# A two-layer transformer kernel on one core: layer 0 with two tiles for low parts, the key bias in the keys' tile, and chain matmuls queued behind the last score

## The chip, the core and the metric

The kernel runs on one core of one Trainium2 chip. A core has several engines, each with its own instruction queue that it works off in order: TensorE (PE in the profile; PEld is its weight load), VectorE (DVE), ScalarE (ACT), GpSimd (POOL) and SyncE (SP), which here issues most of the DMAs. The metric is device time in microseconds of the slowest core; with one core that is the time of the launch. Lower is better.

## The reference

The input `x` is 16 batches of 512 tokens of 128 features, in float32. Two layers follow each other, each of them a half FFN, an attention, and a half FFN again. The change lies in layer 0 alone:

```python
x = x + 0.5 * L0_ffn(layernorm(x))     # silu(gate) * up, inner width 352; all operands
                                       # quantized to 4-bit floats in blocks of 16
x = x + L0_attn(layernorm(x))          # 16 heads of 8; relative positions clipped to +-64
x = x + 0.5 * L0_ffn(layernorm(x))
...                                    # layer 1: another FFN (with experts) and a linear attention

def L0_attn(x):
    dist = clip(k - q, -64, 64) + 64
    q, k, v = heads(x @ W_qkv + b_qkv);  q = q / sqrt(8)
    score = q @ k.T + einsum(q, rel_emb_k[dist])
    attn  = softmax(score, axis=-1)
    ctx   = attn @ v + einsum(attn, rel_emb_v[dist])
    return ctx @ W_out + b_out
```

## The kernel before

**Scores.** A batch is worked in two halves of 256 queries; a half-batch is called a unit here, and its number is u = 2b + half, from 0 to 31. A score tile holds 128 keys by 32 queries of all 16 heads: 128 x 512 numbers in one PSUM tile named `sps`, of which there are three. A unit has 32 such tiles. Each is made twice: once by `maxima`, where VectorE reduces it at once to its maximum over the keys (L341, into `mx`), and once by `main`, where ScalarE takes the exponential (L369, into `PT`). The two lie one unit apart: while `main` works on unit u, `maxima` works on unit u + 1. When its 32 tiles are through, `maxima` gathers the maxima over the tiles (`mk`, L347), turns them on TensorE (L349, also into an `sps` tile), and reduces and negates them on VectorE (L351, L352). The result goes to DRAM (`MD`, L353) and from there into one row of the operand tile `a_BD` (four DMAs, L355), so that the second score comes out with its maximum already subtracted. A score tile is four products of float16 operands (L263: `a_KS` holds the keys, `a_BD` the queries, each as a high and a low part so that the sum has float32's accuracy) and, where the positions are within the clipped range, eight small ones for the relative positions (L267, with `a_TQ` and `a_ET`).

**Projections.** `prep` normalizes a batch, turns it (L282), and makes queries (z = 0) and keys (z = 1) with one product each (L286). Each result is split into a high and a low float16 part by `f16split`: VectorE casts (L143, tile `qkhi`, two buffers), GpSimd subtracts (L144, tile `qklo`, one buffer). Of the queries' parts, copies go into `a_HM` (L298) and from there by twelve DMAs to DRAM (`QM`, L300); high and low parts go by three DMAs each to `QS` and `KSd` (L302). Then the bias that the keys at the clipped distances get is computed from the queries (L305), split by VectorE (L307: `rhi` takes a `qkhi` buffer, `rlo` the `qklo` tile), and stored in `QS` by four DMAs (L309). All of these are on SP's queue for every batch but the first. `loadK` and `load` bring the operands of a unit back on chip in the arrangement that the scores want (L315, L329, L330); they are issued in the middle of the maxima of the unit before.

**What follows the scores.** `main` multiplies the exponentials with the values (L272, L274, into `av`) and with the relative embeddings (`rps`), sends the latter through DRAM to reorder them (`RV`, `RD`, `a_cr`) and copies the former to `cx` (L412). `fin` adds both (L422), turns the sum (L430, four transposes into one `mps` tile; PSUM has two `mps` tiles), divides by the softmax's sum (L433, L434), turns again (L437), multiplies by the output weights (L440) and adds the residual. The FFN halves (`FFN.half`, called `head` ahead of the attention and `tail` behind it) are a chain of the same kind: normalize, quantize (L70 to L81, on VectorE and GpSimd), transpose (L115), two products for each half (L121, L125), quantize, transpose (L133), product (L139).

**Order.** All these are Python generators, and `interleave` runs a step of that one whose due time comes first: `S` in `layer0` lists for each its number of steps and the unit times at which it begins and ends (for example `part`, the stream of maxima, 33 steps per unit; `main` 59 steps; `fin` 5; `head` and `tail` 21; `prep` 11). `prep` runs two batches ahead and `head` three. The tile framework then schedules the traced instructions on each engine by its own timeline; `high_priority` moves an instruction up, and `issue_after(x)` keeps those traced inside it behind x in their engine's queue. Before the main loop, the maxima of unit 0 (`mxs(0,0)`), `FFN1.pre`, `head(1)`, `prep(1)`, the first 14 steps of unit 1's maxima and `head(2)` are traced in this order.

The tile pool `wk` has one buffer for each name unless `bufs` says otherwise, and tiles of one name use the same space in turn: the next use waits until all who read the last one are done. `xn` is such a name too: the normalized batch, then the keys, both [128, 4, 128] float32. `xk` holds the batches' residuals, in seven tiles; `xl` loads one (L474), `tail` stores it (L487) when it is done.

Of the kernel before, what the change touches and what calls it, by code (L numbers as in the profile page):

```python
# [8 lines left out]
F32 = mybir.dt.float32  # L9
F16 = mybir.dt.float16  # L10
# [15 lines left out]
class K:  # L26
# [57 lines left out]
class FFN:  # L84
# [22 lines left out]
    def half(f, xb, half, wk, pp):  # L107
# [6 lines left out]
        ps=pp.tile([128,512],F32,name="mps")  # L114
        for j in range(2): nc.tensor.transpose(ps[:,j*128:(j+1)*128],xq[:,j*128:(j+1)*128],s.ident)  # L115
        xqT=wk.tile([128,256],F32,name="f_x",bufs=3); nc.scalar.copy(xqT,ps[:,:256]); yield
        h=wk.tile([128,2,I],F32,name="f_h")
        for j in range(2):
            t=h[:,j,:]
            g=pp.tile([128,512],F32,name="mps")  # L120
            nc.tensor.matmul(g[:,:I],xqT[:,j*128:(j+1)*128],f.wguT[:,0,:],start=True,stop=True)  # L121
# [3 lines left out]
            nc.tensor.matmul(u[:,:I],xqT[:,j*128:(j+1)*128],f.wguT[:,1,:],start=True,stop=True)  # L125
            nc.vector.scalar_tensor_tensor(t,u[:,:I],0.5,t,ALU.mult,ALU.mult); yield
        for hq in s.quant_steps(h.rearrange("p a b -> p (a b)"),wk,128,44,"hq"): yield
        hq=hq.rearrange("p (a b) -> p a b",a=2)
        for j in range(2):
            ps=pp.tile([128,512],F32,name="mps")  # L130
            for c in range(3):
                P=min(128,I-c*128)
                nc.tensor.transpose(ps[:P,c*128:(c+1)*128],hq[:,j,c*128:c*128+P],s.ident)  # L133
            hT=wk.tile([128,3,128],F32,name="hT",bufs=1)
            nc.scalar.copy(hT[:,0:2,:],ps[:,:256])
            nc.scalar.copy(hT[:96,2,:],ps[:96,256:384])  # L136
            for c in range(3):
                P=min(128,I-c*128)
                nc.tensor.matmul(ps[:,384:512],hT[:P,c,:],f.wdT[:P,c,:],start=(c==0),stop=(c==2),skip_group_check=True)  # L139
            nc.vector.scalar_tensor_tensor(xh[:,j,:],ps[:,384:512],0.5,xh[:,j,:],ALU.mult,ALU.add); yield  # L140
# [5 lines left out]
class Attn0:  # L146
# [110 lines left out]
    def scores(a, out, kt, half, b, BD, TQ, KS):  # L257
# [4 lines left out]
        for g in range(4):  # L262
            nc.tensor.matmul(o4[:,g],KS[:,sd,g*512+kt*128:g*512+(kt+1)*128],BD[:,g,:,b*32:b*32+32].rearrange("p h (x j) -> p x h j",j=4),start=(g==0),stop=(not ib and g==3),skip_group_check=True)  # L263
        if ib:
            for x in range(8):
                w0=kt*128-blk*32-x+a.OFF
                nc.tensor.matmul(out[:,x*64:x*64+64],a.ET[:,w0:w0+128],TQ[:,:,b*32+4*x:b*32+4*x+4],start=False,stop=(x==7),skip_group_check=True)  # L267

# [6 lines left out]
    def prep(a, b, xb, wk, pM):  # L275
# [5 lines left out]
        ps=pM.tile([128,512],F32,name="mps")  # L281
        for j in range(4): nc.tensor.transpose(ps[:,j*128:(j+1)*128],xn[:,j,:],a.ident)  # L282
        xnT=a.xnT[b]=wk.tile([128,512],F32,name="xnT",bufs=2); nc.scalar.copy(xnT,ps); yield
        for z in range(2):
            ps=pM.tile([128,512],F32,name="mps")
            nc.tensor.matmul(ps,a.w[:,z*128:(z+1)*128],xnT,start=True,stop=True)  # L286
            f=wk.tile([128,512],F32,name="qk0") if z==0 else wk.tile([128,4,128],F32,name="xn").rearrange("p a b -> p (a b)")
# [19 lines left out]
        nc.vector.tensor_copy(rhi,ps[:32]); nc.vector.tensor_tensor(rlo,ps[:32],rhi,ALU.subtract)  # L307
# [24 lines left out]
    def maxima(a, b, half, wk, pS, pM):  # L332
# [83 lines left out]
    def fin(a, b, half, X, wk, pM):  # L416
# [11 lines left out]
        for t in range(2):  # L428
            ps=pM.tile([128,512],F32,name="mps")
            for z in range(4): nc.tensor.transpose(ps[:,z*128:z*128+128],cx[:,z,t*128:t*128+128],a.ident)  # L430
            p3=ps.rearrange("p (h c) -> p h c",c=32)
# [4 lines left out]
        ps=pM.tile([128,512],F32,name="mps")  # L436
        for t in range(2): nc.tensor.transpose(ps[:,t*128:t*128+128],cn[:,t,:],a.ident)  # L437
        ct=wk.tile([128,2,128],F32,name="cn").rearrange("p a b -> p (a b)"); nc.scalar.copy(ct,ps[:,:256])
        ps=pM.tile([128,512],F32,name="mps")
        for t in range(2): nc.tensor.matmul(ps[:,t*128:(t+1)*128],ct[:,t*128:(t+1)*128],a.wo,start=True,stop=True)  # L440
        xh=xb[:,2*half:2*half+2,:]
# [15 lines left out]
def layer0(tc, s, w, src, dst, nb=16):  # L457
# [3 lines left out]
    with ExitStack() as c:  # L461
# [56 lines left out]
        loads(1); ffn2(head,1); run(prep(1)); run(part(14)); ffn2(head,2)  # L518
        S=[(part(99999),33*2*nb,W['part'],2*nb+W['part'])]
        for b in range(nb):  # L520
            for h in range(2):
# [7 lines left out]
                if b+hl<nb: at(head(b+hl,h),21,*W['head'])  # L529
                if h==0 and b+pl<nb: at(prep(b+pl),11,*W['prep'])  # L530
# [509 lines left out]
```

## Time and profile before

| | |
|---|---|
| median of 3 runs | 3613.2 us (3611.74 to 3618.94) |
| the profiled execution, its own time | 3625.44 us |
| its span, first to last instruction | 3623.7 us |
| TensorE busy / VectorE / ScalarE / GpSimd, share of the span | 78% / 67% / 47% / 23% |
| mean granted TensorE clock | 0.897 |
| layer 0: first score to last, in the span | 129.4 to 1971.3 us |
| in that stretch: TensorE busy, VectorE busy, clock | 1620.6 us, 1419.7 us, 0.96 |
| behind it (layer 1): TensorE busy, VectorE busy, clock | 1149.1 us, 965.2 us, 0.84 |
| L341 (maximum of a score tile, VectorE) | 1024 of 702 ns |
| L369 (exponential of a score tile, ScalarE) | 1024 of 598 ns |
| L263 (one of a score tile's four products, TensorE) | 8192 of 222 ns |

One execution was profiled, and all single times come from it; it took 12 us longer than the median of the timed runs. The page of the profile gives busy time by engine, then the span in 40 slices of 90.6 us each, in which a digit is the busy share in tenths; the row PEclk is the clock that TensorE was granted, in tenths of full speed. A row of a list of waits reads: engine, what it was about to write, line, what released it, line; then the idle time in us, the number of waits and the longest. In a timeline a row gives the start, the length, the engine, the line and the operation with what it writes and reads; in brackets at its end stands the idle time before it and what ended that. SPq is the issuing of a DMA on SP's queue.

### The profile page before, as it was taken

How to read it: one execution, taken by the hardware profiler on the slowest of the kernel's cores; microseconds unless marked ns; L12 is line 12 of the kernel's file. 1: busy time of each engine (PE TensorE's matmuls, PEld its weight loads, DVE VectorE, ACT ScalarE, POOL GpSimd, SP SyncE). 2: the span in 40 equal slices, each digit the busy share in tenths (PEclk: the TensorE clock that was granted, in tenths of full speed). 3: DMA queues.
4: the chain of work that ended last, by engine and by line, in shares of the span. 5: the costliest groups of instructions: out<-in, count | busy, mean ns of one | idle time of the engine just before them, and what ended most of it. 6: DMA issues, size and time to landing. Idle time of an engine off the chain costs nothing. (4 is left out here: it accounts for less than half of the span.)

```text
span 3623.7 us, 95110 instructions
## 1 busy us (share of the span) xinstructions
PE 2827.4 (78%) x40077; PEld 2034.6 (56%) x40077; DVE 2441.3 (67%) x6508; ACT 1699.9 (47%) x3391; POOL 828.1 (23%) x789
## 2 busy tenths in 40 slices
PE   5579988889888898889896288873788888888470
PEld 3357776767767676677775144431565555555240
DVE  5567878778877787777773467774546655645367
ACT  3144554545445454545554156533455454445242
POOL 4122222222222222222101222212112211111226
PEclk8689999999999999999998589886899989989785
DMA  3232222322223222222210111104312222121401
GB/s 103 59 94 67 58 53 63 80 63 54 62 68 79 63 49 58 75 71 62 53 33 20 32 33 36 36 28 128 90 54 72 62 59 59 36 62 36 128 15 47
DMA packets 290159, 217.23 MB, mean 60 GB/s; under 512 B 77402, under 2 KB 257476, under 8 KB 289604
## 3 DMA queue, kind: packets, MB, share of 16 engines
q1 hardware_dynamic: 284468, 207.72, 21.5%
q8 instruction: 315, 5.16, 0.6%
q10 hardware_dynamic: 5264, 3.43, 0.4%
q14 instruction: 112, 0.92, 0.1%
HBM read 110.28 MB, written 100.78 MB: 58 GB/s over the span
## 5 line engine op out<-in xcount | busy, mean ns | idle before, releaser
L341 DVE TRANSPOSE_TENSOR_REDUCE mx<-sps 128x16 f32<-128x512 f32 x1024 | 702.6, 702 | 221.4 <-PE sps L263 119.5
L369 ACT ACTIVATE PT<-sps 128x512 f32<-128x512 f32 x1024 | 578.4, 598 | 579.0 <-PE sps L263 335.1
L263 PE MATMUL sps<-a_BD,a_KS 128*128 128x128 f16 x8192 | 746.5, 222 | 115.5 <-DVE mx L341 52.1
L263 PEld LDWEIGHTS <-a_KS 128*128 128x128 f16 x8192 | 552.4, 99 | 289.3 <-issue 249.5
L723 DVE SCALAR_TENSOR_TENSOR moe<-mps,oh,moe 128x128 f32<-128x128 f32 x896 | 289.6, 341 | 117.9 <-PE mps L721 104.1
L267 PE MATMUL sps<-a_TQ,a_ET 128*128 128x64 f16 x7168 | 368.5, 194 | 0.4 <-DMA a_TQ<-QM 0.4
L59 POOL TENSOR_TENSOR ln_rs<-ln_ve,negh 128x4 f32<-128x4 f32 (+1 forms) x192 | 174.6, 919 | 636.6 <-DVE ln_ve L58 545.0
L721 PE MATMUL mps<-f_W,T 128*128 128x512 f32 x512 | 298.1, 701 | 26.0 <-DVE moe L723 21.0
L267 PEld LDWEIGHTS <-a_ET 128*128 128x128 f16 x7168 | 309.2, 99 | 1.6 <-DMA a_TQ<-QM 0.6
L79 POOL TENSOR_TENSOR q_M<-f_h,q_M 128x704 f32<-128x704 f32 x64 | 108.2, 1690 | 715.2 <-DVE f_h L78 507.2
L274 PE MATMUL av<-PT,a_V 128*32 128x256 f32 x3840 | 250.7, 386 | 0.0
L896 DVE TENSOR_TENSOR a_at<-pp,a_cm 128x1024 f32<-128x1024 f32 x128 | 154.2, 1214 | 73.1 <-PE pp L894 72.0
L894 PE MATMUL pp<-a_F 64*128 64x128 f32 x2048 | 165.5, 300 | 41.5 <-DVE a_at L896 29.6
L894 PEld LDWEIGHTS pp<-a_F 64*128 64x128 f32 x2048 | 139.6, 202 | 91.6 <-DVE a_at L896 35.0
L721 PEld LDWEIGHTS mps<-f_W,T 128*128 128x128 f32 x512 | 102.1, 223 | 126.7 <-issue 72.9
L274 PEld LDWEIGHTS av<-PT,a_V 128*32 128x32 f32 x3840 | 120.6, 111 | 68.1 <-issue 3.7
L876 ACT ACTIVATE a_F<-pp 128x1024 f32<-128x1024 f32 x128 | 126.6, 1025 | 50.2 <-PE pp L874 44.0
L62 ACT ACTIVATE xn<-xn,ln_mr,ln_rs 128x128 f32<-128x128 f32 x256 | 103.7, 482 | 93.8 <-DVE ln_mr L60 49.0
L274 PE MATMUL rps<-PT,a_TV 128*32 128x64 f32 x6912 | 134.1, 222 | 5.6 <-issue 5.2
L675 ACT COPY f_PT<-St 32x512 f32<-32x512 f32 x128 | 78.7, 615 | 111.2 <-DVE St L674 106.7
L139 PE MATMUL mps<-wdT,hT 128*128 128x128 f32 (+1 forms) x768 | 122.9, 299 | 4.3 <-ACT hT L136 3.6
L874 PE MATMUL pp<-a_QK,a_PK 128*128 128x512 f16 x256 | 81.3, 406 | 55.8 <-DMA a_QK<-a1d 28.9
(348 smaller groups left out, 5375.8 us busy)
## 6 DMA issues: line engine op xcount, KB each, us to landing
QM<-a_HM SPq DMA_DIRECT2D x180, 128.0 KB
a_TQ<-QM SPq DMA_DIRECT2D x120, 192.0 KB
RD<-RV SPq DMA_DIRECT2D x32, 512.0 KB
a_KS<-KSd SPq DMA_DIRECT2D x128, 96.0 KB
a_QK<-a1d SPq DMA_DIRECT2D x128, 96.0 KB
xn<-X SPq DMA_DIRECT2D x32, 256.0 KB
a1d<-a_hi SPq DMA_DIRECT2D x64, 128.0 KB
a_BD<-QS SPq DMA_DIRECT2D x128, 58.0 KB
```

What stands on the lines that cost most here:

```text
L59: nc.gpsimd.tensor_tensor(rs,ve,s.negh[:,:n],ALU.pow); yield
L139: nc.tensor.matmul(ps[:,384:512],hT[:P,c,:],f.wdT[:P,c,:],start=(c==0),stop=(c==2),skip_group_check=True)
L263: nc.tensor.matmul(o4[:,g],KS[:,sd,g*512+kt*128:g*512+(kt+1)*128],BD[:,g,:,b*32:b*32+32].rearrange("p h (x j) -> p x h j",j=4),start=(g==0 ...
L267: nc.tensor.matmul(out[:,x*64:x*64+64],a.ET[:,w0:w0+128],TQ[:,:,b*32+4*x:b*32+4*x+4],start=False,stop=(x==7),skip_group_check=True)
L274: for p,q in mms[1:]: a.nc.tensor.matmul(*p,**q)
L341: with a.s.tc.high_priority(): r=nc.vector.tensor_reduce(mx[:,kt,:,bb],ps.rearrange("p (i c) -> p i c",c=32),axis=AX.X,op=ALU.max,apply_tr ...
L369: nc.scalar.activation(pt[:,:,bb*32:bb*32+32].rearrange("p h (x j) -> p x h j",j=4),ps.rearrange("p (x h j) -> p x h j",x=8,j=4),AF.Exp)
L721: nc.tensor.matmul(ps,yT[:,j*128:(j+1)*128],a.W[:,e2*4:e2*4+4,:],start=True,stop=True)
L723: nc.vector.scalar_tensor_tensor(moe[:,j,:],ps[:,e*128:(e+1)*128],oh[:,j,e2*4+e:e2*4+e+1],moe[:,j,:],ALU.mult,ALU.add)
L876: nc.scalar.activation(f,ps,AF.Relu)
L894: nc.tensor.matmul(ps[:,hh,bs],f[hh*64:hh*64+64,1,bs],f[hh*64:hh*64+64,0,bs],start=True,stop=True)
L896: nc.vector.tensor_tensor(k,ps.rearrange("p h (b q) -> p (h b) q",b=4),a.cm.unsqueeze(1).to_broadcast([128,8,128]),ALU.mult)
```

## The change

The change has four parts. First, `qklo` has two buffers, and the split key bias (`rhi`, `rlo`) lies in a tile of the name `xn`, as [128, 1024] float16, in place of a `qkhi` buffer and the `qklo` tile. Second, `scores` remembers its last matmul (`s.lastmm`), and a new function `gate()` puts the matmuls of the chains (projections, FFN, `fin`, the transpose of `mk`) behind the last score traced so far in TensorE's queue; the values' product (L319) and those of `main` (L272, L274) are not gated. Third, three `yield`s are added, in the FFN between the copy of `hT` and its product, in `maxima` ahead of the transpose of `mk`, and in `fin` ahead of the output product; the numbers of steps follow. Fourth, `xk` has six tiles where it had seven. The same instructions are issued as before. In the diff the other gated matmuls are left out: in `half` all of L115 to L139, in `prep` L282 too, in `fin` L430, L437 and L440.

```diff
+    lastmm=None
+    def gate(s):
+        return s.tc.issue_after(s.lastmm) if s.lastmm is not None else ExitStack()
...
     def half(f, xb, half, wk, pp):
...
-        for j in range(2): nc.tensor.transpose(ps[:,j*128:(j+1)*128],xq[:,j*128:(j+1)*128],s.ident)
+        with s.gate():
+            for j in range(2): nc.tensor.transpose(ps[:,j*128:(j+1)*128],xq[:,j*128:(j+1)*128],s.ident)
...
             hT=wk.tile([128,3,128],F32,name="hT",bufs=1)
             nc.scalar.copy(hT[:,0:2,:],ps[:,:256])
-            nc.scalar.copy(hT[:96,2,:],ps[:96,256:384])
+            nc.scalar.copy(hT[:96,2,:],ps[:96,256:384]); yield
...
     def scores(a, out, kt, half, b, BD, TQ, KS):
...
-            nc.tensor.matmul(o4[:,g],KS[...],BD[...],...)
+            r=nc.tensor.matmul(o4[:,g],KS[...],BD[...],...)
...
+        a.s.lastmm=getattr(r,"ins",r)
...
     def prep(a, b, xb, wk, pM):
...
-            nc.tensor.matmul(ps,a.w[:,z*128:(z+1)*128],xnT,start=True,stop=True)
+            with s.gate(): nc.tensor.matmul(ps,a.w[:,z*128:(z+1)*128],xnT,start=True,stop=True)
...
-            hi=wk.tile([128,512],F16,name="qkhi",bufs=2); lo=wk.tile([128,512],F16,name="qklo")
+            hi=wk.tile([128,512],F16,name="qkhi",bufs=2); lo=wk.tile([128,512],F16,name="qklo",bufs=2)
...
-        nc.tensor.matmul(ps[:32],a.eb.rearrange("p a b -> p (a b)"),q,start=True,stop=True)
-        rhi=wk.tile([128,512],F16,name="qkhi",bufs=2)[:32]; rlo=wk.tile([128,512],F16,name="qklo")[:32]
+        with s.gate(): nc.tensor.matmul(ps[:32],a.eb.rearrange("p a b -> p (a b)"),q,start=True,stop=True)
+        r=wk.tile([128,1024],F16,name="xn"); rhi=r[:32,:512]; rlo=r[:32,512:]
...
     def maxima(a, b, half, wk, pS, pM):
...
+        yield
         ps=pS.tile([128,512],F32,name="sps")
-        nc.tensor.transpose(ps[:,:128],mk.rearrange("p s b x -> p (s b x)"),a.ident)
+        with a.s.gate(): nc.tensor.transpose(ps[:,:128],mk.rearrange("p s b x -> p (s b x)"),a.ident)
...
     def fin(a, b, half, X, wk, pM):
...
-        ct=wk.tile([128,2,128],F32,name="cn").rearrange("p a b -> p (a b)"); nc.scalar.copy(ct,ps[:,:256])
+        ct=wk.tile([128,2,128],F32,name="cn").rearrange("p a b -> p (a b)"); nc.scalar.copy(ct,ps[:,:256]); yield
...
 def layer0(tc, s, w, src, dst, nb=16):
...
-        xk=c.enter_context(tc.tile_pool(name="xk",bufs=7))
+        xk=c.enter_context(tc.tile_pool(name="xk",bufs=6))
...
-        S=[(part(99999),33*2*nb,W['part'],2*nb+W['part'])]
+        S=[(part(99999),34*2*nb,W['part'],2*nb+W['part'])]
...
-                at(A.fin(b,h,X,wk,pM),5,1+fn[0],1+fn[1])
-                at(tail(b,h),21,1+fn[1]+.001,1+fn[1]+tl)
+                at(A.fin(b,h,X,wk,pM),6,1+fn[0],1+fn[1])
+                at(tail(b,h),23,1+fn[1]+.001,1+fn[1]+tl)
```

More of the change, by code (lines that the diff above doesn't have):

```diff
@@ L120, in half @@
             g=pp.tile([128,512],F32,name="mps")
-            nc.tensor.matmul(g[:,:I],xqT[:,j*128:(j+1)*128],f.wguT[:,0,:],start=True,stop=True)
+            with s.gate(): nc.tensor.matmul(g[:,:I],xqT[:,j*128:(j+1)*128],f.wguT[:,0,:],start=True,stop=True)
             nc.scalar.activation(t,g[:,:I],AF.Tanh,scale=0.5)
@@ L124, in half @@
             u=pp.tile([128,512],F32,name="mps")
-            nc.tensor.matmul(u[:,:I],xqT[:,j*128:(j+1)*128],f.wguT[:,1,:],start=True,stop=True)
+            with s.gate(): nc.tensor.matmul(u[:,:I],xqT[:,j*128:(j+1)*128],f.wguT[:,1,:],start=True,stop=True)
             nc.vector.scalar_tensor_tensor(t,u[:,:I],0.5,t,ALU.mult,ALU.mult); yield
@@ L130, in half @@
             ps=pp.tile([128,512],F32,name="mps")
+            with s.gate():
+                for c in range(3):
+                    P=min(128,I-c*128)
+                    nc.tensor.transpose(ps[:P,c*128:(c+1)*128],hq[:,j,c*128:c*128+P],s.ident)
+            hT=wk.tile([128,3,128],F32,name="hT",bufs=1)
+            nc.scalar.copy(hT[:,0:2,:],ps[:,:256])
+            nc.scalar.copy(hT[:96,2,:],ps[:96,256:384]); yield
             for c in range(3):
                 P=min(128,I-c*128)
-                nc.tensor.transpose(ps[:P,c*128:(c+1)*128],hq[:,j,c*128:c*128+P],s.ident)
-            hT=wk.tile([128,3,128],F32,name="hT",bufs=1)
-            nc.scalar.copy(hT[:,0:2,:],ps[:,:256])
-            nc.scalar.copy(hT[:96,2,:],ps[:96,256:384])
-            for c in range(3):
-                P=min(128,I-c*128)
-                nc.tensor.matmul(ps[:,384:512],hT[:P,c,:],f.wdT[:P,c,:],start=(c==0),stop=(c==2),skip_group_check=True)
+                with s.gate(): nc.tensor.matmul(ps[:,384:512],hT[:P,c,:],f.wdT[:P,c,:],start=(c==0),stop=(c==2),skip_group_check=True)
             nc.vector.scalar_tensor_tensor(xh[:,j,:],ps[:,384:512],0.5,xh[:,j,:],ALU.mult,ALU.add); yield
@@ L262, in scores @@
         for g in range(4):
-            nc.tensor.matmul(o4[:,g],KS[:,sd,g*512+kt*128:g*512+(kt+1)*128],BD[:,g,:,b*32:b*32+32].rearrange("p h (x j) -> p x h j",j=4),start=(g==0),stop=(not ib and g==3),skip_group_check=True)
+            r=nc.tensor.matmul(o4[:,g],KS[:,sd,g*512+kt*128:g*512+(kt+1)*128],BD[:,g,:,b*32:b*32+32].rearrange("p h (x j) -> p x h j",j=4),start=(g==0),stop=(not ib and g==3),skip_group_check=True)
         if ib:
@@ L266, in scores @@
                 w0=kt*128-blk*32-x+a.OFF
-                nc.tensor.matmul(out[:,x*64:x*64+64],a.ET[:,w0:w0+128],TQ[:,:,b*32+4*x:b*32+4*x+4],start=False,stop=(x==7),skip_group_check=True)
+                r=nc.tensor.matmul(out[:,x*64:x*64+64],a.ET[:,w0:w0+128],TQ[:,:,b*32+4*x:b*32+4*x+4],start=False,stop=(x==7),skip_group_check=True)
+        a.s.lastmm=getattr(r,"ins",r)
     xnT={}; pend={}; last=None
@@ L281, in prep @@
         ps=pM.tile([128,512],F32,name="mps")
-        for j in range(4): nc.tensor.transpose(ps[:,j*128:(j+1)*128],xn[:,j,:],a.ident)
+        with s.gate():
+            for j in range(4): nc.tensor.transpose(ps[:,j*128:(j+1)*128],xn[:,j,:],a.ident)
         xnT=a.xnT[b]=wk.tile([128,512],F32,name="xnT",bufs=2); nc.scalar.copy(xnT,ps); yield
@@ L429, in fin @@
             ps=pM.tile([128,512],F32,name="mps")
-            for z in range(4): nc.tensor.transpose(ps[:,z*128:z*128+128],cx[:,z,t*128:t*128+128],a.ident)
+            with s.gate():
+                for z in range(4): nc.tensor.transpose(ps[:,z*128:z*128+128],cx[:,z,t*128:t*128+128],a.ident)
             p3=ps.rearrange("p (h c) -> p h c",c=32)
@@ L436, in fin @@
         ps=pM.tile([128,512],F32,name="mps")
-        for t in range(2): nc.tensor.transpose(ps[:,t*128:t*128+128],cn[:,t,:],a.ident)
-        ct=wk.tile([128,2,128],F32,name="cn").rearrange("p a b -> p (a b)"); nc.scalar.copy(ct,ps[:,:256])
+        with s.gate():
+            for t in range(2): nc.tensor.transpose(ps[:,t*128:t*128+128],cn[:,t,:],a.ident)
+        ct=wk.tile([128,2,128],F32,name="cn").rearrange("p a b -> p (a b)"); nc.scalar.copy(ct,ps[:,:256]); yield
         ps=pM.tile([128,512],F32,name="mps")
-        for t in range(2): nc.tensor.matmul(ps[:,t*128:(t+1)*128],ct[:,t*128:(t+1)*128],a.wo,start=True,stop=True)
+        with s.gate():
+            for t in range(2): nc.tensor.matmul(ps[:,t*128:(t+1)*128],ct[:,t*128:(t+1)*128],a.wo,start=True,stop=True)
         xh=xb[:,2*half:2*half+2,:]
@@ L525, in layer0 @@
                 fn,tl=(W['fin'],W['tail']) if u<2*nb-2 else ((.3,.5),.6)
-                at(A.fin(b,h,X,wk,pM),5,1+fn[0],1+fn[1])
-                at(tail(b,h),21,1+fn[1]+.001,1+fn[1]+tl)
+                at(A.fin(b,h,X,wk,pM),6,1+fn[0],1+fn[1])
+                at(tail(b,h),23,1+fn[1]+.001,1+fn[1]+tl)
                 if h==1 and b+hl+1<nb: at(xl(b+hl+1),1,-.35,-.3)
-                if b+hl<nb: at(head(b+hl,h),21,*W['head'])
+                if b+hl<nb: at(head(b+hl,h),23,*W['head'])
                 if h==0 and b+pl<nb: at(prep(b+pl),11,*W['prep'])
```

## The prediction

> **What bounds the kernel now.** I read the page first, then the table of windows, the waits of TensorE, and the timeline around the longest wait.
>
> ```profile
> span 3623.7 us, 95110 instructions
> PE   5579988889888898889896288873788888888470
> PEclk8689999999999999999998589886899989989785
> ```
>
> Layer 0, the only part that changes, is slices 1 to 22 (its first score starts at 129.4 us, its last at 1971.3). TensorE is at 8 or 9 tenths there, with its clock at 9.
>
> ```profile
> 600.00:800.00 200.00, 182.05 (x3296) 143.24 (x3294) 161.29 (x352) 104.95 (x229) 43.17 (x43) 0.97 0.25 63
> 915.00:921.50 6.50, 0.86 (x7) 0.29 (x4) 1.32 (x3) 1.08 (x2) 4.16 (x3) 0.95 0.42 117
> 921.50:927.00 5.50, 5.50 (x51) 4.97 (x52) 4.01 (x11) 2.06 (x4) 0.00 (x0) 0.50 0.13 12
> ```
>
> Columns: window, length, busy time of PE, PEld, DVE, ACT, POOL, granted clock, DMA share, GB/s. In 200 us TensorE works 182 and VectorE 161, so TensorE is the bound and VectorE is close behind. In the 6.5 us at 915 everything stands still; in the 5.5 us after it TensorE is busy at half clock. The waits say what stood in the way:
>
> ```profile
> PE mps L430 <- DVE qklo L307: 60.2, 11, 7.0
> PE sps L263 <- DVE mx L341: 46.2, 121, 9.4
> PE sps L263 <- ACT PT L369: 27.0, 58, 2.5
> ```
>
> 60.2 us in 11 waits of up to 7.0, one in each batch of 115 us; all other waits but a few are under 1.2 us. The timeline of one of them:
>
> ```profile
> 905.88 8.76 SPq L300 DMA_DIRECT2D QM<-a_HM  x12
> 914.68 0.60 SPq L302 DMA_DIRECT2D QS<-qklo  x1
> 917.21 1.15 POOL L144 TENSOR_TENSOR qklo<-xn,qkhi 128x512 f16<-128x512 f32 x1 [20.64 <-DMA QS<-qklo]
> 918.39 0.52 SPq L302 DMA_DIRECT2D KSd<-qklo  x1
> 920.76 0.68 DVE L307 TENSOR_TENSOR qklo<-mps,qkhi 32x512 f16<-32x512 f32 x1 [5.18 <-DMA KSd<-qklo]
> 921.50 1.12 PE L430 MATMUL mps<-ident,cx 128*128 128x128 f32 x4 [5.64 <-DVE qklo L307]
> 924.47 1.37 SPq L353 DMA_DIRECT2D MD<-mn  x2
> 930.66 1.30 SPq L355 DMA_DIRECT2D a_BD<-MD  x2
> ```
>
> One qklo tile serves three uses in turn: the queries' low part, the keys', the key bias's. The second waits until the first has been stored, behind twelve QM stores on SP (914.68 to 917.21); the third until the second has been stored (918.39 to 920.76). VectorE stands at L307, its score reductions queue behind that, and L430 needs the PSUM tile that L307 reads.
>
> **The change, part by part.**
>
> *Two qklo tiles, bias in the keys' tile.* Each use has its own tile, so POOL's L144 for the keys can follow the query's work at once, and L307 waits only for it (1.15 us) and for its own matmul. Of the 11 waits nothing is left: −60.2, and −1.8 for two short ones at L437. The bias also leaves qkhi, so L307's cast no longer waits for QS<-qkhi: in batch 2 that wait let TensorE stand 9.4 us.
>
> ```profile
> 259.98 0.68 DVE L307 CAST qkhi<-mps 32x512 f16<-32x512 f32 x1 [8.82 <-DMA QS<-qkhi]
> 129.43 0.58 PE L263 MATMUL sps<-a_BD,a_KS 128*128 128x128 f16 x4 [16.73 <-DMA a_BD<-QS]
> ```
>
> Together −71. In batch 0 L307 ended at 100.7 after a wait of 4.81; 3 of it would go, and the first score (129.43, above, which waits for what is stored after L307) comes at 126: −3.
>
> *The half clock.* After each of 12 long waits TensorE works some 5.5 us at 0.50. There the mean score matmul takes 0.31 us in place of 0.22, so 5.5 x (1 − 0.22/0.31) = 1.6 us each: −19. The Trainium skill, "TensorE: Matmul & The Clock Gate", section "HAM oscillation — how this bites in real kernels", counts throttled time times one half, which would be 33 in place of 19 and a total 14 lower; the rows decide here, since these matmuls slowed by 1.4 only. Its section "A second HAM failure mode: psum-queue depth-cycling" speaks against the change, which adds short waits for PSUM tiles: by it many micro-idles could bring the half clock back. In the trace 46 + 27 us of such waits leave windows like 600 to 800 at 0.97.
>
> *The gates in steady state.* No instruction is added; the same matmuls stand later. By the order of both programs the query/key products of a batch move some 25 scores later, onto the maxima's end; fin's and FFN's move 5 to 20. What is new is bunching on VectorE. From one batch's last maximum (M31) to the eighth of the next (M7), VectorE's queue held, beside 8 reductions of 0.65, about 9 us of other work (L307 0.68, L347 2 x 0.53, FFN and fin pieces); now it holds the copies L143 and L298 (0.4 + 0.75), more of the FFN's L123, L70 to L78 and both L307: about 13.5. So 19 us of VectorE where it was 15, against some 15 us of TensorE queued there (four FFN products of 0.83, L286 2 x 1.1, L305 1.04, L430 1.3, av 1.9, rps 1.1, 18 scores of 0.24 to 0.47). Elsewhere VectorE has less to do and TensorE sets the pace. Three score tiles take up about 2 us of the 4; I take 2 a batch, 13 batches: +26. Bounds: 4 a batch (+52), and −13, which is all the time TensorE now waits at chain matmuls other than L430's long waits (8.6 for cx, 5.2 for mk).
>
> *Start-up.* The gate binds hardest before the main loop. Before, the FFN of batch 1 and the projections of batch 1 ran between the first 46 scores:
>
> ```profile
> 181.70 1.96 PE L286 MATMUL mps<-xnT,a_w 128*128 128x512 f32 x4
> 184.52 0.57 SPq L302 DMA_DIRECT2D QS<-qkhi  x1
> 217.33 0.39 PE L263 MATMUL sps<-a_BD,a_KS 128*128 128x128 f16 x4
> 222.67 0.58 PE L263 MATMUL sps<-a_BD,a_KS 128*128 128x128 f16 x4 [4.95 <-issue]
> ```
>
> From the store QS<-qkhi to the flow of batch 1's scores it takes 222.67 − 184.52 = 38 us (38 DMAs on SP). Now the first 32 maxima run bare: 126 + 32 x 0.64 + 1.1 for L347 = 148. Then come 32 more (20.5), the two FFN halves of batch 1 (10.5 us of VectorE each, 4 of it done earlier) and L347: 39 us, at the 85% that VectorE was busy there 45: 193. L286 of batch 1 stands behind that, and on SP its stores stand behind MD<-mn (1.5 after L349) and the four a_BD<-MD that wait for it (6.2 + 2.5, as at 924.47 and 930.66): QS<-qkhi at 203, scores at 241, some 18 later. The FFN of batch 2 fills TensorE meanwhile but nothing that ends sooner. I take +16; bounds +8 (SP not held by MD) and +25 (the FFN chain slower).
>
> *Last batch.* At 1935.9 L430 held TensorE 9.91 us for cx; now nine scores and one av (5 to 7 us) stand ahead of it: −5, bounds −10 and 0.
>
> *At nothing:* the yields and step counts (pacing alone); six x tiles for seven: a load of x now stands on SP behind the store that frees its tile and waits for its landing, 2.4 us by the KSd<-qklo row; the QS stores behind it are due some 15 scores later, which covers it (2.4 x 13 = 31 without that cover). Layer 1: its code is the same, 0.
>
> Sum: −71 − 3 − 19 + 26 + 16 − 5 = −56. The profiled execution took 3625.4 (span 3623.7 and 1.7 around it), 12 above the median of 3613.2; the terms are carried over as they are: **3557**. Its own range, by the bounds of gates and start-up: 3525 to 3592.
>
> **Rivals.**
>
> *The gates cost nothing* (bunching 0, start-up +8): −90, 3523. For it: the 60 us wait stopped all engines, so its removal gives work back to all. Against: VectorE at 161 of 200 has little room for bunching.
>
> *The gain is eaten:* VectorE's stretch costs the full 4 a batch and each such wait brings 1.6 of half clock, (5.6 − 2) x 13 = +47: 3604; with start-up at its bound 3613, no change. For it: some places show a dip of the clock after waits of 1.2 to 2.5 us.
>
> *Slower:* a new wait takes the place of the old, at the first exponential of every second half-batch. MD<-mn stood on SP ten microseconds after the QM burst; in the new order it stands right behind it, since L286 and L349 now come together. From QS<-qkhi (904.57 to 916.57 with twelve QM), KSd<-qklo, MD, 6.2 to a_BD<-MD, four of those and about 2.1 to land, the row arrives 23 us after QS<-qkhi. The first score that needs it stands about 25 us of TensorE work after L349, which starts 1 us before that store. So the margin is about a microsecond. If the row came 6 us late in 13 batches, with 1.6 of half clock each, that is +99: 3656. It decides from 56/13 = 4.3 us of lateness a batch.
>
> **How the numbers follow.** Forecast 0.62, gates free 0.18, gain eaten 0.11, slower 0.09. A measurement of this kernel can tell 0.2% from no change, 3606 to 3620. Faster: the first two, and half of the third, 0.86; same 0.05; slower 0.09. The range 3518 to 3608 leaves out the slower case and the edges of two others.
>
> **What would show it.** Right: L430 <- L307 gone from the waits; POOL's 20 us for QS<-qklo gone; the period from one L305 to the next 108 to 111 us where it was 115; first batch-1 scores at 230 to 245; clock near 0.99 in mid-layer. Wrong: L307 still waiting, now for POOL's L144 behind another quantization; long ACT waits at the first score of a half-batch behind a_BD<-MD; L263 <- L341 grown well past 46 us.

## The result and the profile after

The changed kernel takes 3664.15 us (median of 4 runs, 3655.35 to 3669.95) where the kernel before takes 3614.11 (4 runs in all): a ratio of 1.0138, with an interval of 1.0123 to 1.0153. It is 50 us slower; 57 us faster was forecast. Line numbers of layer 0 have moved: the score product L263 is L269 now, the maximum L341 is L350, the exponential L369 is L379, the bias split L307 is L316, and `fin`'s three steps on TensorE, L430, L437 and L440, are L441, L449 and L453.

The page of the changed kernel, span, TensorE and clock:

```profile
span 3653.6 us, 95142 instructions
PE   5568888888898888889887288872788788888570
PEclk8889999999999999999999589885899899999785
```

The profile shows a run that took 3655.35 us. TensorE is at 8 or 9 tenths through most of layer 0 as before, and its clock is at 9 there; in the second slice it is at 8 where it was at 6. The waits of TensorE from 180 to 1920 us (engine, what it writes, line, releaser; total, times, longest):

```profile
PE sps L269 <- DVE mx L350: 70.6, 142, 1.5
PE sps L269 <- ACT PT L379: 32.4, 85, 1.2
PE rps L280 <- ACT RV L413: 20.3, 12, 4.4
PE sps L269 <- DMA a_BD<-QS: 18.8, 1, 18.8
PE mps L449 <- DVE xn L316: 15.2, 12, 1.3
PE av L280 <- ACT PT L379: 15.1, 32, 0.7
```

The long wait of before, 60.2 us in 11, is gone, as forecast. In its place stand waits of about a microsecond: for score tiles (70.6 where it was 46.2, 32.4 where it was 27.0), for the copies of `rps`, for the bias's cast, for the exponentials. One long wait is new, 18.8 us at the start.

To place the difference I use the end of the last exponential of a unit (from the trace). Before, unit 7 ends at 643.3 and unit 23 at 1566.3: (1566.3 - 643.3)/8 = 115.4 us a batch, called the period below. Changed: (1577.2 - 656.3)/8 = 115.1. So the wait is gone and the period in the middle of layer 0 is the same. The changed kernel is 5.5 us behind at the end of unit 1 (308.5 against 303.0), 13.0 at that of unit 7, 10.9 at unit 23 and 19.3 at unit 31 (1992.0 against 1972.7). The rest of this profile's 30 us comes behind layer 0: 1661.6 us from there to the end of the span, before 1651.0.

### The profile page after: what moved, and what is told of

Its sections match the earlier page's. It is cut to its first block, busy times and chain, and to the rows that moved or that the text cites. A ratio compares the mean times of both kernels' runs of the same rounds, so it can differ in the third digit from the quotient of the medians.

```text
span 3653.6 us, 95142 instructions
## 1 busy us (share of the span) xinstructions
PE 2824.9 (77%) x40077; PEld 2031.9 (56%) x40077; DVE 2433.3 (67%) x6508; ACT 1703.6 (47%) x3391; POOL 842.6 (23%) x789
## 5 line engine op out<-in xcount | busy, mean ns | idle before, releaser
L350 DVE TRANSPOSE_TENSOR_REDUCE mx<-sps 128x16 f32<-128x512 f32 x1024 | 701.9, 701 | 339.8 <-PE sps L269 176.7
L269 PE MATMUL sps<-a_BD,a_KS 128*128 128x128 f16 x8192 | 742.6, 221 | 179.0 <-DVE mx L350 74.9
L379 ACT ACTIVATE PT<-sps 128x512 f32<-128x512 f32 x1024 | 579.6, 599 | 499.6 <-PE sps L269 280.8
L269 PEld LDWEIGHTS <-a_KS 128*128 128x128 f16 x8192 | 551.5, 98 | 329.8 <-issue 292.9
L83 POOL TENSOR_TENSOR q_M<-f_h,q_M 128x704 f32<-128x704 f32 x64 | 107.4, 1678 | 737.4 <-DVE hq_sc L75 344.2
L282 PE MATMUL av<-PT,a_V 128*32 128x256 f32 x3840 | 247.6, 382 | 0.0
L282 PEld LDWEIGHTS av<-PT,a_V 128*32 128x32 f32 x3840 | 119.8, 110 | 66.3 <-issue 0.9
L688 ACT COPY f_PT<-St 32x512 f32<-32x512 f32 x128 | 78.7, 615 | 110.2 <-DVE St L687 104.4
L282 PE MATMUL rps<-PT,a_TV 128*32 128x64 f32 x6912 | 127.7, 221 | 2.9 <-issue 2.9
L413 ACT COPY RV<-rps 128x128 f32<-128x128 f32 x256 | 67.9, 419 | 129.5 <-PE rps L282 85.6
```

Source lines behind the costliest of these rows:

```text
L269: r=nc.tensor.matmul(o4[:,g],KS[:,sd,g*512+kt*128:g*512+(kt+1)*128],BD[:,g,:,b*32:b*32+32].rearrange("p h (x j) -> p x h j",j=4),start=(g= ...
L282: for p,q in mms[1:]: a.nc.tensor.matmul(*p,**q)
L350: with a.s.tc.high_priority(): r=nc.vector.tensor_reduce(mx[:,kt,:,bb],ps.rearrange("p (i c) -> p i c",c=32),axis=AX.X,op=ALU.max,apply_tr ...
L379: nc.scalar.activation(pt[:,:,bb*32:bb*32+32].rearrange("p h (x j) -> p x h j",j=4),ps.rearrange("p (x h j) -> p x h j",x=8,j=4),AF.Exp)
```

## The experiments

Each run is compared by its ratio to the kernel before, run beside it; a ratio's interval reaches 0.1 to 0.3% to either side. The runs come from several rounds, and the changed kernel, run in two of them, gave ratios 0.3% apart, so smaller differences between rounds are not read. A period comes from one profile of each kernel.

| kernel | ratio | period, us |
|---|---|---|
| before | 1 | 115.4 |
| changed; the same again | 1.0138; 1.0166 | 115.1; 116.6 |
| the tiles alone | 0.9768 | 108.9 |
| gates, yields and counts alone | 1.0203 | 118.1 |
| changed, without gates | 1.0021 | 117.1 |
| changed, gates from the main loop on | 1.0051 | 117.2 |
| changed, without yields | 0.9947 | 111.2 |
| tiles and the FFN's yield | 0.9910 | 111.4 |
| tiles and the yield of `mk` | 0.9697 | 106.4 |
| tiles and `fin`'s yield | 0.9855 | 110.6 |
| changed, without the FFN's yield | 0.9822 | 108.5 |
| changed, without `fin`'s yield | 1.0146 | 117.3 |
| before with six x tiles | 1.0016 | 115.6 |
| changed, FFN's yield in, count 21 | 0.9842 | 108.9 |
| changed, FFN's yield out, count 23 | 1.0127 | 117.3 |
| changed, FFN's yield out, gates from the main loop on | 0.9746 | 108.8 |
| before with the bias tile alone | 1.0021 | 115.0 |
| tiles and `mk`'s yield, FFN paced as 23 | 0.9917 | 113.2 |
| tiles and `mk`'s yield, FFN paced as 19 | 0.9872 | 111.9 |

**The parts.** First question: did the wait not matter (another limit holds 115 us a batch), or was a real gain given back?

The tiles alone:

```diff
-lo=wk.tile([128,512],F16,name="qklo")
+lo=wk.tile([128,512],F16,name="qklo",bufs=2)
-rhi=...name="qkhi",bufs=2)[:32]; rlo=...name="qklo")[:32]
+r=wk.tile([128,1024],F16,name="xn"); rhi=r[:32,:512]; rlo=r[:32,512:]
-name="xk",bufs=7
+name="xk",bufs=6
```

> The kernel before with the tiles alone: two qklo tiles, the bias in an xn tile, six x tiles; no gates, no yields. Theory A (the gain of the tiles is real, about 5 us of wait and 1.6 of half clock a batch, and the gates give it back): the L307 wait goes, the period of a batch falls from 115.3 to about 109.5, and the time to about 3535 us (70 to 90 less). Theory B (the period of 115.3 is held by something else, VectorE's 92 us of work a batch and the ring of three score tiles, so that an idle stretch that goes comes back as many small ones): the period stays within 1 us of 115.3 and the time at 3600 to 3620.

Measured 0.9768 (0.9742 to 0.9794), period 108.9: theory A. In the stretch shown further on, TensorE's queue holds the same order in this kernel and in the one before, so 6.5 us a batch is what the tiles are worth by themselves.

Gates, yields and counts, with the tiles as before (the six x tiles stay):

```diff
-lo=...name="qklo",bufs=2)
+lo=...name="qklo")
-r=wk.tile([128,1024],F16,name="xn"); rhi=r[:32,:512]; rlo=r[:32,512:]
+rhi=...name="qkhi",bufs=2)[:32]; rlo=...name="qklo")[:32]
```

> The changed kernel with the tiles as before (one qklo, the bias in qkhi and qklo): gates, yields and counts alone. Theory A: the gates cost about 5.5 us a batch by themselves, and with the L307 wait still there the period goes to about 120 and the time to about 3730 us. Theory B: the period stays at 115 to 116 and only start and end (some 20 us) and layer 1 (10) remain: 3640 to 3665.

Measured 1.0203 (1.0178 to 1.0229), period 118.1: slower than before by itself, but less than theory A's 3730. The expectation was wrong in one point: TensorE has no L316 wait in the main loop here, but a single one of 6.0 us. VectorE's own wait at this line for the store `KSd<-qklo`, 58.1 us in 12 in layer 0 before, is 1.0 us in one here, so the new order takes away the same wait as the tiles do; which of the moved products does it was not tried. In this order the tiles are worth only 0.4 to 0.65% (1.0203 against 1.0166 and 1.0138); the worths of the parts do not simply add.

Without the gates, everything else as changed:

```diff
-return s.tc.issue_after(s.lastmm) if s.lastmm is not None else ExitStack()
+return s.tc.issue_after(s.lastmm) if 0 else ExitStack()
```

> The changed kernel without the gates: tiles, yields, step counts and six x tiles as in it. Theory A: like the tiles alone, 3535, give or take 10 for the yields. Theory B: 3600 to 3620. If the yields are what costs, it stays near 3660.

Measured 1.0021 (1.0004 to 1.0038), period 117.1. On 3614 us that is 3622, near theory B's number, and yet it is not theory B, since the tiles alone gave 0.9768: three yields and four step counts alone eat 2.5%. In this kernel `fin`'s sum runs beside the quantization on GpSimd, and TensorE waits for it. Its timeline (start, length, engine, line):

```profile
674.79 1.38 POOL L85 TENSOR_TENSOR q_M<-q_M,hq_sc 128x704 f32<-128x704 f32 x1
675.23 2.91 DVE L432 TENSOR_TENSOR cx<-cx,a_cr 128x512 f32<-128x512 f32 x2
678.20 1.12 PE L441 MATMUL mps<-ident,cx 128*128 128x128 f32 x4 [1.41 <-DVE cx L432]
```

Gates from the main loop on:

```diff
-    lastmm=None
+    lastmm=None; gates_on=False
+        s.gates_on=True          # ahead of S=[...]
-... if s.lastmm is not None else ExitStack()
+... if s.lastmm is not None and s.gates_on else ExitStack()
```

> The changed kernel with the gates switched on only from the main loop, so that what is traced before it is ordered as before. The first unit's last exponential ended 21.9 us later in the changed kernel, the second's 5.5 later. Both theories: if the start is a cost by itself it goes: 8 to 15 us less than the changed kernel, 3650 to 3656. If it is made up for by the second unit anyway, no difference: 3660 to 3668.

Measured 1.0051 (1.0032 to 1.0071): less than the changed kernel, by more than expected. Unit 1 ends at 289.2 in place of 308.5, and by unit 23 both stand at 1577. One profile could not say whether that was the start's price; a later run does. The kernel without gates, of the same round, is at 1.0021: with the yields in, gates in the main loop cost 0.3%, some 11 us.

**Which yield.** All three out, counts as before:

```diff
-nc.scalar.copy(hT[:96,2,:],ps[:96,256:384]); yield
+nc.scalar.copy(hT[:96,2,:],ps[:96,256:384])
...     # mk, fin likewise; 34 -> 33, 6 -> 5, 23 -> 21
```

> The changed kernel without its three yields and with the step counts of before: tiles, gates and six x tiles. Against the kernel before in the same runs (the tiles alone gave a ratio of 0.977, the changed kernel 1.014, the tiles with the yields 1.002). Theory Y (the yields give the gain back, the gates cost only at the start and the end, some 25 us): ratio about 0.983, period of a batch near 109. Theory G (the gates bunch VectorE's work, 5 us a batch, with or without the yields): ratio 1.000 to 1.010, period near 114.

Measured 0.9947 (0.9931 to 0.9963), period 111.2: between the two. On the tiles, the gates cost 0.9947 - 0.9768 = 1.8% and the yields another 1.9 to 2.2.

Each yield on the tiles alone, with its count:

> The tiles and, of the yields, only that in the FFN, with its 23 steps. In the tiles with all yields TensorE waited 38.8 us in eight batches at L441 for the sum cx on VectorE (4.4 with the tiles alone), where the sum ran beside the quantization on GpSimd and took 1.9 us in place of 1.1. Theory H (the FFN's new pacing puts the two side by side): nearly all of the 88 us, ratio 0.995 to 1.005, period near 117. Rival (it is another yield, or all of them together): ratio 0.975 to 0.983.

> The tiles and only the yield ahead of the transpose of mk, 34 steps a unit. Theory H: nothing to speak of, ratio 0.975 to 0.980. Rival: the row of maxima arrives later and the maxima are paced anew, ratio above 0.99.

> The tiles and only the yield in fin, 6 steps. Theory H: nothing to speak of, ratio 0.975 to 0.980. Rival: fin's later steps move by a sixth of its stretch, and its sum is asked for earlier than VectorE has it: a wait at L430 for cx of 4 to 5 us a batch and a ratio above 0.99.

Measured 0.9910 (0.9881 to 0.9939), 0.9697 (0.9667 to 0.9726) and 0.9855 (0.9825 to 0.9884). The FFN's costs 1.4% and is the largest, but not "nearly all"; `fin`'s costs 0.9; that of `mk` gains 0.7, which nobody expected, and makes the fastest kernel of all. Singly they add up to 1.6%, together they cost 2.5.

Left out singly from the changed kernel, which was run again beside them:

> The changed kernel as it is, beside the others of this call and on their chip: ratio 1.012 to 1.016, period of a batch 115 again. If its profile differs from the first by more than 10 us in the stretch of unit 7 to 23, single profiles are not to be read to a microsecond a batch.

> The changed kernel without the FFN's yield (21 steps): tiles, gates, the yields of mk and fin. Without any yield the ratio was 0.995 and the period 111.2; with all three 1.014 and 115.1. Theory H (the FFN's yield is the bulk under the gates too, as on the tiles alone, where it cost 2.5 us a batch, fin's 1.7, and mk's gained 2.6): ratio 0.990 to 0.998, period 110.5 to 112. Rival (with the gates it matters little, the gates set where the FFN's products stand): 1.008 to 1.014.

> The changed kernel without fin's yield (5 steps): tiles, gates, the yields of the FFN and mk. Theory H: 1.000 to 1.008, period 113 to 114.5. Rival (fin's yield is the one that costs under the gates): 0.990 to 0.998.

Measured 1.0166 (1.0138 to 1.0194), 0.9822 (0.9793 to 0.9852) and 1.0146 (1.0121 to 1.0170). The FFN's yield with its count is 3.4% under the gates, all of the loss and more; `fin`'s is nothing there. The two profiles of the changed kernel differ by 11.5 us between unit 7 and unit 23, and by 15 behind layer 0 (1661.6 and 1677.0): beyond the bound set, so a single profile is not read to a microsecond a batch, and the 10 us that layer 1 seemed to lose in the first one are not put down to the change.

**Split or pace.** The yield does two things: it parts a step, and its count of 23 makes all earlier steps of the FFN due earlier. One kernel has the yield and the old count, the other the reverse:

```diff
-tail(b,h),23 ... head(b+hl,h),23
+tail(b,h),21 ... head(b+hl,h),21      # FFN's yield, count 21
...
-nc.scalar.copy(hT[:96,2,:],ps[:96,256:384]); yield
+nc.scalar.copy(hT[:96,2,:],ps[:96,256:384])      # count 23, no FFN's yield
```

> The changed kernel with the FFN's yields left in but its step count back at 21, so that each step is due as before and the last two pairs run late. With 23 and the yields the ratio was 1.014 to 1.017 and the period 115 to 116.6; without both 0.982 and 108.5. Theory P (the pace: with 23 the FFN's early steps are due earlier, and its four gate and up products, with VectorE's work behind them, fall into the stretch around the end of the maxima, where the batch loses 5 of its 6.6 us): 0.980 to 0.990, period 108 to 110.5. Theory S (the split: the PSUM tile and the two tiles hT and f_h are held over another step): 1.005 to 1.017, period 113 to 117.

> The changed kernel without the FFN's yields but with the count of 23, so that 21 steps are due at the pace of 23. Theory P: 1.005 to 1.017, period 113 to 117. Theory S: 0.980 to 0.990.

Measured 0.9842 (0.9819 to 0.9865), period 108.9, and 1.0127 (1.0108 to 1.0147), period 117.3. It is the pace; the split costs nothing that these runs can tell. The count by itself costs some 3%: 1.0138 and 1.0166 against 0.9842 with the yield in, 1.0127 against 0.9822 with it out.

Where the pace costs is seen in windows. The stretch runs from the 16th exponential of a batch's first half to its 32nd; the end of the maxima of the second half, `mk`, the projections, `fin` and FFN products lie in it. The last lines give sums over 8 batches and their means over them, first for the kernel before, then for the tiles alone, for the changed kernel without the FFN's yield, and for the changed kernel (each a fence of its own; one window of each is shown ahead of the sum: window, length, busy time of PE, PEld, DVE, ACT, POOL, granted clock, DMA share, GB/s):

```profile
905.20:941.40 36.20, 27.67 (x395) 21.36 (x390) 26.15 (x61) 13.28 (x31) 8.53 (x7) 0.91 0.42 106
...
sum 288.20, PE 222.64 PEld 169.40 DVE 208.13 ACT 106.10 POOL 68.22; mean PE 27.83 PEld 21.17 DVE 26.02 ACT 13.26 POOL 8.53
```

```profile
866.30:896.50 30.20, 25.25 (x397) 19.02 (x390) 26.48 (x63) 12.87 (x31) 7.44 (x6) 1.00 0.50 119
...
sum 236.30, PE 205.66 PEld 153.44 DVE 207.47 ACT 103.86 POOL 58.83; mean PE 25.71 PEld 19.18 DVE 25.93 ACT 12.98 POOL 7.35
```

```profile
889.30:920.60 31.30, 27.00 (x393) 18.93 (x381) 28.01 (x52) 14.90 (x32) 7.15 (x5) 1.00 0.35 90
...
sum 251.80, PE 217.41 PEld 152.00 DVE 223.95 ACT 119.15 POOL 57.16; mean PE 27.18 PEld 19.00 DVE 27.99 ACT 14.89 POOL 7.14
```

```profile
916.00:952.70 36.70, 30.70 (x414) 22.60 (x403) 32.58 (x67) 16.12 (x35) 12.71 (x9) 0.95 0.31 80
...
sum 293.90, PE 247.70 PEld 182.23 DVE 259.81 ACT 128.02 POOL 101.19; mean PE 30.96 PEld 22.78 DVE 32.48 ACT 16.00 POOL 12.65
```

Divide by 8. Before, the stretch lasts 36.0 us with 26.0 of VectorE's work: 72%, the L307 wait lies in it. With the tiles it lasts 29.5 for the same work: 88%. In the changed kernel without the FFN's yield it is 31.5 with 28.0, 89%; in the changed kernel 36.7 with 32.5, 88%. So once the wait is gone VectorE is the busiest engine of this stretch, at 88 to 89%, and what is moved into it lengthens it: the FFN's yield with its count brings in 4.5 us of VectorE's work and 5.3 us of time. The gates by themselves do the same on a smaller scale; here are the sums of the tiles with the gates and no yields:

```profile
sum 260.80, PE 225.85 PEld 157.06 DVE 234.53 ACT 121.40 POOL 57.04; mean PE 28.23 PEld 19.63 DVE 29.32 ACT 15.17 POOL 7.13
```

That is 32.6 us with 29.3 of VectorE's work, 90%. That VectorE sets the length is the likelier reading, not shown. TensorE is nearly as busy (25.7 of 29.5, 27.2 of 31.5, 31.0 of 36.7: 87, 86 and 84%), and the same move brings it 3.8 us more work. In the changed kernel's window shown, 4.0 of TensorE's 6.0 us of idle time end with VectorE, yet VectorE too waits there for TensorE's scores. The kernel without gates goes the other way: against the tiles alone its stretch has 0.4 us more of VectorE's work and 1.8 more of TensorE's (26.3 and 27.5 us), and takes 2.3 us longer. No run gave the stretch more of VectorE's work alone.

The rest of the batch, up to the 16th exponential of the next, does not get it back. Its sums, without the FFN's yield and changed:

```profile
sum 617.20, PE 576.25 PEld 480.82 DVE 502.69 ACT 360.02 POOL 156.42; mean PE 72.03 PEld 60.10 DVE 62.84 ACT 45.00 POOL 19.55
```

```profile
sum 628.80, PE 566.44 PEld 463.12 DVE 465.34 ACT 349.99 POOL 124.78; mean PE 70.81 PEld 57.89 DVE 58.17 ACT 43.75 POOL 15.60
```

VectorE has 4.7 us less to do there, but it was not the busiest: TensorE is busy 72.0 of 77.1 us and 70.8 of 78.6. Why this part grows by 1.45 us, with less work for both engines, stays open.

**The smaller terms.** Six x tiles alone:

```diff
-name="xk",bufs=7
+name="xk",bufs=6
```

> The kernel before with six x tiles in place of seven, nothing else. As predicted, nothing: ratio 0.998 to 1.002. If a load that waits for a store on SP holds the queries' stores behind it, up to 31 us: 1.008.

Measured 1.0016 (1.0004 to 1.0028): some 6 us, within the range expected.

The bias tile alone (one `qklo`, seven x tiles):

```diff
-rhi=...name="qkhi",bufs=2)[:32]; rlo=...name="qklo")[:32]
+r=wk.tile([128,1024],F16,name="xn"); rhi=r[:32,:512]; rlo=r[:32,512:]
```

> The kernel before with the key bias in an xn tile and nothing else: one qklo tile for the queries and the keys, seven x tiles. The two tiles and the bias together gave 0.977. If VectorE's wait at the bias is what cost (GpSimd may wait, it has time): the bias alone gives nearly all of it, 0.976 to 0.982. If GpSimd's wait of 20 us for the queries' low part holds up others: less than half, 0.989 to 1.0.

Measured 1.0021 (1.0002 to 1.0040): no gain at all, outside both guesses. Its waits between unit 7 and unit 23:

```profile
PE mps L430 <- DVE xn L307: 38.9, 8, 6.6
...
DVE xn L307 <- POOL qklo L144: 38.4, 8, 6.4
...
POOL qklo L144 <- DMA QS<-qklo: 168.2, 8, 23.8
```

The wait only changed its name. The bias overwrites the keys in `xn`, so VectorE waits until GpSimd has made their low part, and that waits for the one `qklo` tile as before. So the bias's tile needs the second `qklo` tile beside it. The second `qklo` tile alone was not run.

The gates at the start, priced without the FFN's yield:

> The changed kernel without the FFN's yields, count 21, and with the gates only from the main loop on. The second unit's last exponential ended at 310.8 with the gates from the start and at about 290 in every kernel without them: if the start is a cost by itself, 16 to 20 us less than 0.982, so 0.976 to 0.978. If the main loop takes it back: 0.981 to 0.983.

Measured 0.9746 (0.9728 to 0.9764) against 0.9822: 0.8%, some 27 us (the two intervals leave 15 to 40); in the profiles unit 1 ends at 291.5 in place of 310.8, 19 us.

The pace on the fastest kernel, which has no gates:

```diff
-tail(b,h),21 ... head(b+hl,h),21
+tail(b,h),23 ... head(b+hl,h),23      # and in the other kernel 19
```

> The tiles and the yield of mk, without gates (ratio 0.970, period 106.4, the fastest so far), with the FFN's 21 steps paced as 23. If the pace costs by where it puts the FFN's work against the maxima's end, with or without gates: 0.985 to 1.005, period 109 to 114. If only gated products suffer from it: 0.967 to 0.975.

> The same with the FFN's 21 steps paced as 19, later in place of earlier. If slower is better still, below 0.967; if 21 happens to lie well and any shift brings other collisions, 0.975 to 0.995.

Measured 0.9917 (0.9890 to 0.9944) and 0.9872 (0.9849 to 0.9895), against 0.9697 at 21. So the pace costs without gates too, and in both directions: of the three counts 21 is the best, and slower isn't better. Where it costs differs. Paced as 19, the stretch goes from 29.5 to 33.3 us, with VectorE's work in it from 26.3 to 29.5 (88%), and the rest of the batch from 76.8 to 78.7. Paced as 23, the stretch goes to 31.4 us only, and the rest of the batch to 81.9. What stands behind that I did not settle.

## Why the prediction was wrong, step by step

**The tiles, -71 - 3, and the half clock, -19: right in the main.** Together 93 us were forecast; the tiles alone gave 0.9768, 84 us of 3614, with the six x tiles in it. There L430's wait for L307 falls from 60.2 to 3.1 us, GpSimd's 20 us wait for `QS<-qklo` is gone, and the clock between unit 7 and unit 23 rises from 0.96 to 0.99. The stretch's sums tell the two terms apart: TensorE's idle time there falls by 4.4 us a batch (8.2 to 3.8), where the waits were put at 5.5, and its busy time by 2.1 (27.8 to 25.7), where the half clock was put at 1.6. The 3 us at the start did not come: the first score begins at 128.3 us with the tiles alone and at 130.0 in the changed kernel, before at 129.4.

The rule of the Trainium skill that spoke against the change, "A second HAM failure mode: psum-queue depth-cycling" in "TensorE: Matmul & The Clock Gate", shows in part. Between unit 7 and unit 23 the changed kernel, with its many short waits, has a clock of 0.98. But in the stretch the clock is below 1.00 in six of its eight windows (0.91 to 0.95), with the tiles alone in three (0.94), without the FFN's yield in one (0.95). By the windows' clocks that is some 3.8 us of half clock a batch against 1.3 with the tiles; at the prediction's 0.31 us for 0.22 the difference is worth 0.7 us a batch, an estimate. In each of the six the dip follows a wait of 1.27 us at L449 for the bias's cast (L316); in the other two the same wait is followed by none. The waits for score tiles do not bring it by themselves: without the FFN's yield TensorE waits more for score tiles in the stretch (2.6 us a batch against 1.8) and the clock holds in seven of eight.

**The gates in steady state, +26: right for tiles and gates, 2 us a batch.** Tiles and gates without yields have a period of 111.2 where the tiles have 108.9, so 2.3 a batch by two profiles; by the ratios the gates cost 1.8%, 65 us, of which the start takes 27, and 38 in 16 batches is 2.4. The place fits too: the stretch has 3.4 us more of VectorE's work and takes 3.1 us longer. But the price hangs on the rest of the order. With the yields of `mk` and `fin` in, the gated kernel's period is 108.5, no longer than that of the tiles alone; with all yields in, gates in the main loop cost 0.3%.

**The start, +16: the chain right, the price low by the ratios.** The first scores of batch 1 were put at 241 us, 18 later than before, and the timeline of the changed kernel has

```profile
241.80 1.01 PE L269 MATMUL sps<-a_BD,a_KS 128*128 128x128 f16 x8 [18.83 <-DMA a_BD<-QS]
```

The cost is 19 us by the profiles and 27 by the ratios (15 to 40), against bounds of 8 and 25. Ahead of the very first score TensorE now stands 34.5 us, where it stood 16.7, since the FFN of batch 1 has moved behind the scores. In the changed kernel itself the ratios make it 31 us (1.0138 against 1.0051).

**The last batch, -5: it did not come.** The wait that it named, 9.91 us at L430 for `cx`, is gone in the changed kernel; TensorE's longest wait in the last 190 us of layer 0 is now 6.7 us, for GpSimd at L120. Yet the two batches from unit 27 to unit 31 take 92.5 us each with the tiles, 93.6 with the gates added, and 96.9 in the changed kernel, where they took 93.4 before; without the FFN's yield they take 92.3.

**"At nothing: the yields and step counts (pacing alone)": the step that failed.** The forecast missed by 107 us. The FFN's yield with its count is worth 3.4%: 1.0166 with both, 0.9822 without, on kernels run side by side. On 3614 us that is 124 us; the count by itself is some 3%, about 110 us. A step count issues no instruction, but it decides when each FFN step is due, hence which work shares a stretch with the maxima's end. The prediction had looked at that place, and at VectorE's bunching in it, for the gates alone, at 2 us a batch; by the periods it is 2.3 for the gates and 4 to 5.4 more for the yields (111.2 against 115.1 and 116.6). `mk`'s yield, also put at nothing, gained 0.7% on the tiles.

Without the FFN's yield and count the changed kernel stands at 0.9822 x 3614 = 3550, beside the forecast of 3557. That nearness is partly luck: the gates' steady cost does not show in that kernel, while the start cost more than forecast.

**Two other sums of the prediction are off.** By its own bounds (-13 for the gates, +8 for the start) the lower end of "its own range" is 3510, not 3525. And the "some 15 us" of TensorE's work queued at the maxima's end is the low end of its own list: with 18 scores of 0.24 to 0.47 it adds up to 15 to 19. Neither explains the miss, which is on the slow side.

**Rivals.** None of them happened as described. The slower one named a late `MD<-mn` at the first exponential; TensorE's waits in the changed kernel have no line for `a_BD<-MD` at all. "The gain is eaten" had the right place, VectorE's stretch, but only for the gates, and with a cap of 4 us a batch: the changed kernel lies 115.1 - 108.9 = 6.2 above the tiles. Of the signs of being wrong, one stands in the profile: TensorE's waits for score tiles that VectorE holds, 70.6 us where they were 46.2.

## What to carry to other kernels

A pacing number in a generator schedule is an edit like any other: find the stretch where a second engine is already near its limit, and count how much of its work the new due times bring in. Price it by that stretch's own row (VectorE at 88% of its length), not by the span, where VectorE was at 67%; time moved out of the rest of the batch, where TensorE was the busiest, was not given back here. Such a count only says where to look: paced as 23 on the tiles with `mk`'s yield, most of the cost came in the rest of the batch. Try parts singly: here tiles (0.977), gates (+1.8% on the tiles), one yield (-0.7% on the tiles) and one count (+3% under the gates) were bundled; they do not simply add, and the best version, the tiles with the yield of `mk`, is 3% faster than the kernel before.

## What the runs showed of the hardware

Two kinds of VectorE instruction grow long beside GpSimd, by nearly as much as GpSimd still has to run. The two instructions of `fin`'s sum (L432), in the timeline of the kernel without gates shown above, took 2.91 us together where GpSimd's L85 runs for the first 0.94 (674.79 + 1.38 - 675.23); in the changed kernel, with GpSimd idle, such a pair took 2.09:

```profile
923.46 2.09 DVE L432 TENSOR_TENSOR cx<-cx,a_cr 128x512 f32<-128x512 f32 x2
```

None of the 64 instructions of this sum meets GpSimd in the changed kernel, and each takes 1.07 to 1.15 us. Without gates 36 of them meet L85 and take 1.9 to 2.3 us; the other 28 take 1.08 to 1.15. In the changed kernel the negation `mn`, 128x32 numbers, 0.17 us before, took 1.46 beside GpSimd's copy into `a_HM`, and both end together; its timeline:

```profile
930.83 1.76 POOL L307 COPY a_HM<-qklo 128x512 f16<-128x512 f16 x1
931.16 1.46 DVE L362 TENSOR_SCALAR mn<-mt 128x32 f16<-128x32 f32 x1
```

The maxima do not grow: four of them beside GpSimd's L83, in the kernel without gates, took 2.50 us, 0.63 each.

```profile
672.81 2.50 DVE L350 TRANSPOSE_TENSOR_REDUCE mx<-sps 128x16 f32<-128x512 f32 x4
673.04 1.67 POOL L83 TENSOR_TENSOR q_M<-f_h,q_M 128x704 f32<-128x704 f32 x1 [2.49 <-DVE f_h L82]
```

The Trainium skill, "SBUF — State Buffer", section "Who interferes with whom", has a rule for both: VectorE and GpSimd share a pair of ports, which an instruction of VectorE with two inputs in SBUF, and a `tensor_scalar` in some of its modes, contend for with GpSimd; the pair is locked, so the one that comes second waits. The rows agree. No run here took such a meeting away by itself, so what it costs the kernel stays open.
